# Starting a scan direction's preparation one block earlier in the SSD stage of a four-layer Mamba / ConvNeXt kernel

## The chip, the cores and the metric

The kernel runs on one core of a Trainium2 chip. The metric is the device time of one launch in microseconds (us), from the first to the last instruction of the core. A core has five engines that run side by side, each with its own list of instructions in a fixed order: PE (TensorE, matmuls; PEld is its weight load), DVE (VectorE), ACT (ScalarE), POOL (GpSimd) and SP (SyncE), which here issues all the DMAs. They wait for one another by semaphores.

## What is computed

The input is a float32 image batch (4, 96, 64, 64). It passes through four layers: a two-layer Mamba block with fusion and batch statistics, an SSD (Mamba-2) layer, another Mamba block, and a ConvNeXt block (7x7 depthwise convolution, layer norm, MLP). Only the SSD layer matters here. Cut to its core it is

```python
xn = rmsnorm(x)                                  # over channels, per pixel
xs = stack([xn, flip(xn), swap(xn), flip(swap(xn))])   # four scan directions, 4096 tokens each
z, xBC, dt = split(xs @ in_proj_w.T)             # 192, 192 + 128 + 128, 3 heads
dt  = softplus(dt + dt_bias)                     # step sizes, one per token and head
xBC = silu(conv_b + causal_conv4(xBC))           # x, B, C
dAc = cumsum(dt * A)  within a chunk
y   = tril(C B^T * exp(dAc_s - dAc_t)) * dt @ x  +  C exp(dAc) @ state  +  D * x
state = exp(dAc_last) * state + sum(exp(dAc_last - dAc) * dt * B x)
out = unscan(rmsnorm(y * silu(z)) @ out_proj_w.T) / 4 + residual
```

The decay factors of a whole direction depend on `dt` alone, and so on `xn` alone: they can be made before the direction's scan starts.

## The kernel before, in words

The program is written in a tile framework: the program's order gives each instruction its priority, a scheduler puts the instructions of each engine into a list, and tiles of a pool with one name share a ring of `bufs` buffers. A tile that takes a buffer of its ring waits until the readers of the buffer's tile before have finished.

`Ssd.run` (line 986) works through 16 directions: 4 images `b`, two orientations `o` (rows, columns), and two senses `r` (0 forward, 1 backward). A direction has four blocks of 1024 tokens, a block eight chunks of 128 tokens (`Q`), so 512 chunks in all. The loop of line 1021 runs over the chunks `n` and issues for each the recurrent work, in a software pipeline: `sums_to` (line 846, one DMA per pair of chunks that spreads the decay rows over the partitions, four chunks ahead), `decay` (856, two ahead), `weights` (869, one ahead), `outputs` (888), then `scale`, `by_channels` and `finish`. Line 931, in `outputs`, is a Square on ACT that runs once per chunk.

Two Python generators are advanced between these stages.

- `front` (line 780) makes the inputs of the next block: for `r` = 0 first `z` (16 matmul instructions, L796), then B and C (24, L814), then x (48, L825), then a Silu and the transposes of B. It is advanced four times per chunk (eight times where the next block is the first of a forward direction) and drained at the block's last chunk. Its PSUM tiles come from `bank("front")`, a ring of two.
- `prelude` (line 763) prepares the next direction. It exists once per direction, and its parts are:

```python
if r == 0:
    yield from self.rmsnorm(b) if o == 0 else self.turn()   # 8 steps
    yield from self.step_sizes(o)                           # 8 rows, a DMA read, the softplus
self.seq[b, o, r] = self.decays(r)
```

`rmsnorm` (666) loads and normalises an image into `xn[0]`; `turn` (685) copies `xn[0]` transposed to `xn[1]` on POOL. `step_sizes` (696) makes eight rows of `dt` (matmul L706, ACT copy L711, DMA L712 to a DRAM tile), reads them back in another shape (DMA L717), takes the softplus (from L719) and transposes the result (L725). `decays` (729) makes the cumulative sums (L743, L745), their exponentials, `coef` (L751 to L753) and the decay rows in DRAM (L756, L758, DMA L760). These matmuls too write to `bank("front")`: one tile for L725, one for L743 and L745 (read last by L748), one for L756. The tiles `dac`, `dec`, `edac`, `coef` of `decays` have two buffers each, so that those of a direction overwrite those of two directions before.

For a forward direction (`r` = 0) the prelude has 18 yields and so needs 19 calls of `next`; for a backward one it has none and one call does it all. Lines 1028 to 1033 decide when it is called: once per chunk from a first block on, and whatever is left is run at once at the last chunk of the third block (n = 23 of the direction ahead of it). The block after that is the one in which `front` makes the first block of the new direction.

Of the kernel before, what the change touches and what calls it, by code (L numbers as in the profile page):

```python
# [65 lines left out]
QB = BLK // Q  # L66
# [207 lines left out]
class Scan:  # L274
# [108 lines left out]
    def run(self, steps, wts, front, first):  # L383

        units = [(j, q, p) for j in range(3) for q in range(NQU) for p in range(2)]
        made = [first] + [{} for _ in steps[1:]]
        groups = [
            dict(
                pair=pair, sub=sub, c=c, wt=wts[sub], made=made[n], j=j, q=q, half=p, quarters=(p, p + 2),
                first=(q == 0 and p == 0), last=(q == NQU - 1 and p == 1),  # L390
                dma=(q % 2 == 0 and p == 1),
            )
            for n, (pair, sub, c) in enumerate(steps) for j, q, p in units
        ]
        total, each = len(groups), len(units)
        ahead = iter(())
        for n in range(-4, total + 6):
            slot = (n + LEAD) % each
            if slot == 0:
                for _ in ahead:  # L400
                    pass
                step = (n + LEAD) // each + 1
                ahead = front(step, made[step]) if step < len(steps) else iter(())

            def at(lag):
                return groups[n - lag] if 0 <= n - lag < total else None

            if (g := at(3)) and g["last"]:
                self.close(g)
            for stage, lag in (  # L410
                (self.load, -4), (self.spread, -1), (self.decay, -2), (self.scan, 0), (self.sums, 2),
            ):
                if g := at(lag):
                    stage(g)

            for lag, what in ((4, self.project), (5, self.fuse)):
                if (g := at(lag)) and g["last"] and g["j"] and (g["sub"] or lag == 4):
                    what(g, g["j"] - 1)
            for _ in range(PACE[slot] if slot < len(PACE) else 0):
                next(ahead, None)  # L420
# [152 lines left out]
class Ssd:  # L573
# [412 lines left out]
    def run(self):  # L986
        nblk = L // BLK
        steps = [
            (b, o, r, blk if r == 0 else nblk - 1 - blk)
            for b in range(B) for o in range(2) for r in range(2) for blk in range(nblk)  # L990
        ]
        made = [{} for _ in steps]
        chunks = []
        for n, (b, o, r, blk) in enumerate(steps):
            for m in range(QB):
                pair = {} if m % 2 == 0 else pair
                chunks.append(dict(
                    b=b, o=o, r=r, blk=blk, c=m if r == 0 else QB - 1 - m, made=made[n], pair=pair,
                    first=(m == 0 and n % nblk == 0), last=(m == QB - 1 and n % nblk == nblk - 1),
                    second=(m % 2 == 1),  # L1000
                ))

        def front(n):
            if n >= len(steps):
                return iter(())
            return self.front(*steps[n], made[n], steps[n + 1] if n + 1 < len(steps) else None)


        preludes = [
            (n, self.prelude(*steps[n][:3])) for n in range(0, len(steps), nblk)  # L1010
        ]
        first = preludes.pop(0)[1]
        for _ in range(2):
            next(first)
        self.weights_of(self.w)
        for _ in first:
            pass
        self.switch(0)
        for _ in front(0):
            pass  # L1020
        for n in range(-4, len(chunks) + 4):
            def at(lag):
                return chunks[n - lag] if 0 <= n - lag < len(chunks) else None

            m = n // QB + 1
            if n % QB == 0 and n >= 0:
                ahead = front(m)
            if n >= 0 and preludes and n // QB >= preludes[0][0] - 3:
                if n == (preludes[0][0] - 1) * QB - 1:
                    for _ in preludes.pop(0)[1]:  # L1030
                        pass
                else:
                    next(preludes[0][1], None)


            extra = m < len(steps) and steps[m][2:] == (0, 0)
            for point, stage in enumerate(("weights", "outputs", "finish", "decay")):
                if stage == "weights" and n >= 0 and n % QB == QB - 1 and m < len(steps):
                    while "silu" not in made[m]:
                        next(ahead)  # L1040
                if stage == "weights" and (g := at(-1)):
                    self.weights(g)
                if stage == "outputs" and (g := at(0)):
                    self.outputs(g)
                if stage == "outputs" and (g := at(1)) and g["second"]:
                    self.scale(g)
                if stage == "weights" and (g := at(3)) and g["second"]:
                    self.finish(g)
                if stage == "finish" and (g := at(2)) and g["second"]:
                    self.by_channels(g)  # L1050
                if stage == "decay" and (g := at(-4)) and not g["second"]:
                    self.sums_to(g)
                if stage == "decay" and (g := at(-2)):
                    self.decay(g)
                if n >= 0:
                    for _ in range(2 if extra else 1):
                        next(ahead, None)
            if n % QB == QB - 1 and n >= 0:
                for _ in ahead:
                    pass  # L1060
        self.switch(None)
# [250 lines left out]
```

## Time and profile before

| | us |
|---|---|
| three runs, median (lowest, highest) | 10018.94 (10013.64, 10032.7) |
| profiled run | 10004.88 |
| span of its core | 10002.8 |
| PE busy in the span | 8588.6 (86%) |
| DVE busy | 8164.7 (82%) |
| POOL busy | 6969.7 (70%) |
| ACT busy | 5524.9 (55%) |
| granted TensorE clock, mean | 0.935 |

The SSD layer lies in the middle, from 3068.6 to 6245.7 us. A window of the profile gives, for a stretch of time, the busy time of each engine with the count of its instructions, the clock that TensorE was granted (1.00 is full speed), the mean busy share of the DMA engines and what they moved in GB/s. A line of the timeline gives start, duration, engine (a `q` behind the name is the engine's sequencer, as for issuing a DMA), line of the code, the operation, the tiles written and read, and in brackets how long the engine had been idle and who ended that. Busy time is an average over stages with different limits, so the SSD stage is read by itself.

### The profile page before, as it was taken

What the parts mean: (1) busy time and instruction counts of PE and PEld (TensorE: products, weight loads), DVE (VectorE), ACT (ScalarE), POOL (GpSimd) and SP (SyncE); (2) the same over time, 40 slices, a digit from 0 to 9 for tenths busy, and PEclk for the clock granted to TensorE, in tenths of its full rate; (3) what the DMA queues carried; (4) which work ended last, traced back from release to release, by engine and by line L of the source; (5) the groups of instructions that cost most, each with busy time, mean ns of one, the idle gap of its engine ahead of it and who ended that gap; (6) DMA issues with size and microseconds to landing.
All of it is one profiled execution on the core that took longest, in us unless ns stands there. A gap on an engine that the chain in (4) does not pass through costs nothing. (4 is left out here: it accounts for less than half of the span.)

```text
span 10002.8 us, 109739 instructions
## 1 busy us (share of the span) xinstructions
PE 8588.6 (86%) x32744; PEld 3547.4 (35%) x32744; DVE 8164.7 (82%) x10861; ACT 5524.9 (55%) x10500; POOL 6969.7 (70%) x4600
## 2 busy tenths in 40 slices
PE   7888888888886988988998888788888888888688
PEld 1222222222213676776776766122121222221122
DVE  7999999999994666666656667799999999999787
ACT  5666666656653455545545544566666665665244
POOL 6888888888884555555555555688888888888322
PEclk9999999999997999999999999899999999999798
DMA  7777777777773223222312321767777777777442
GB/s 188 199 202 202 203 208 207 201 201 206 200 201 113 70 68 95 67 66 83 84 60 74 86 66 53 189 197 206 205 201 205 208 201 202 205 205 198 113 99 73
DMA packets 803534, 1528.27 MB, mean 153 GB/s; under 512 B 124253, under 2 KB 128249, under 8 KB 802170
## 3 DMA queue, kind: packets, MB, share of 16 engines
q1 hardware_dynamic: 802938, 1521.25, 54.7%
q8 instruction: 260, 4.26, 0.2%
q14 instruction: 336, 2.75, 0.1%
HBM read 1229.69 MB, written 156.37 MB: 139 GB/s over the span
## 5 line engine op out<-in xcount | busy, mean ns | idle before, releaser
L342 POOL TENSOR_TENSOR hc<-hs,bc 128x1024 f32<-128x1024 f32 x1536 | 3607.7, 2355 | 625.0 <-DVE hs L340 555.7
L340 DVE TENSOR_TENSOR_SCAN hs<-da,carry,bs 128x512 f32<-128x512 f32 x2016 | 2467.2, 1265 | 79.6 <-DVE bs L335 1.9
L107 ACT ACTIVATE da<-da,w_a 128x512 f32<-128x512 f32 x2304 | 1616.0, 716 | 1272.5 <-DMA da<-dd 1212.9
L361 PE MATMUL py<-hc,selsum 128*32 128x512 f32 x6144 | 1794.2, 636 | 472.8 <-POOL hc L342 462.9
L313 PE MATMUL bs<-du,seldu 64*128 64x512 f32 x4608 | 1578.0, 678 | 203.9 <-DVE hs L340 190.8
L335 DVE TENSOR_TENSOR bs<-bs,bc 128x1024 f32<-128x1024 f32 x1152 | 1398.3, 1214 | 189.3 <-PE bs L313 187.5
L308 POOL TENSOR_TENSOR du<-du,bc 128x1024 f32<-128x1024 f32 x384 | 904.4, 2355 | 289.6 <-DMA du<-dg 170.0
L361 PEld LDWEIGHTS py<-hc,selsum 128*32 128x32 f32 x6144 | 240.0, 110 | 1818.5 <-POOL hc L342 1119.0
L313 PEld LDWEIGHTS bs<-du,seldu 64*128 64x128 f32 x4608 | 446.5, 196 | 1205.2 <-DVE hs L340 859.4
L879 POOL TENSOR_TENSOR seg<-seg,cb 128x384 f32<-128x384 f32 x512 | 514.1, 1005 | 511.2 <-DVE cb L878 389.1
L194 PE MATMUL pu<-h,w_conv 96*128 96x512 f32 (+3 forms) x2048 | 834.5, 628 | 6.8 <-ACT rs L107 6.5
L863 DVE TENSOR_SCALAR seg<-dr,dac 128x128 f32<-128x128 f32 x1536 | 618.5, 435 | 265.1 <-PE y L908 248.0
L340 DVE TENSOR_TENSOR_SCAN hs<-bs,carry,du 128x512 f32<-128x512 f32 x672 | 823.8, 1260 | 8.5 <-issue 5.2
L814 PE MATMUL front<-pk,sconv 128*128 128x512 f32 x1536 | 750.2, 607 | 11.9 <-ACT z L802 7.5
L883 POOL TENSOR_TENSOR xs<-pre,coef 128x576 f32<-128x576 f32 x512 | 598.1, 1173 | 200.8 <-PE halves L922 144.4
L918 POOL TENSOR_TENSOR y<-y,xs 128x192 f32<-128x192 f32 x496 | 294.3, 593 | 546.7 <-DVE y L917 543.6
L931 ACT ACTIVATE y<-yz 128x192 f32<-128x192 f32 x512 | 186.1, 364 | 864.1 <-DVE yz L930 863.1
L825 PE MATMUL front<-sconv,pk 128*128 128x192 f32 x3072 | 573.8, 330 | 50.5 <-DVE pre L830 43.1
L1175 DVE SCALAR_TENSOR_TENSOR acc<-pad,c_conv,acc 96x1024 f32<-96x1024 f32 x336 | 491.4, 1467 | 112.1 <-ACT acc L1166 61.2
L345 ACT COPY carry<-hs 128x2 f32<-128x2 f32 x1344 | 250.5, 186 | 561.0 <-DVE hs L340 558.1
L825 PEld LDWEIGHTS front<-sconv,pk 128*128 128x128 f32 x3072 | 498.6, 191 | 81.1 <-DVE pre L830 68.9
L107 ACT ACTIVATE bs<-da,w_a 128x512 f32<-128x512 f32 x768 | 522.0, 680 | 2.3 <-DVE hs L340 0.7
(196 smaller groups left out, 13919.2 us busy)
## 6 DMA issues: line engine op xcount, KB each, us to landing
da<-dd SPq DMA_DIRECT2D x3072, 256.0 KB
du<-dg SPq DMA_DIRECT2D x768, 256.0 KB
dr<-rows SPq DMA_DIRECT2D x256, 384.0 KB
bc<-rows SPq DMA_DIRECT2D x256, 256.0 KB
dd<-delta SPq DMA_DIRECT2D x192, 256.0 KB
dg<-du SPq DMA_DIRECT2D x192, 256.0 KB
pk<-xn SPq DMA_DIRECT2D x128, 384.0 KB
pk<-xn SPq DMA_DIRECT2D x128, 256.0 KB
```

The source lines that it names most:

```text
L107: self.last = self.scalar.activation(out, in_, func, **kw)
L194: nc.tensor.matmul(pu[r0:r1], lhsT=wt["conv"][:kk, tap, d0:d1], rhs=h[:kk, b, ds(tap, T)], start=(tap == 0), stop=(tap == 3),)
L308: nc.gpsimd.tensor_tensor(g["du"], g["du"], self.b_or_c(g, 0), ALU.mult)
L313: nc.tensor.matmul(g["bs"][:, i], lhsT=self.sel["du"][rows, g["half"], g["q"]], rhs=g["made"]["du"][rows, g["j"]], start=True, stop=True,)
L335: nc.vector.tensor_tensor(dbx, dbx, self.b_or_c(g, 0), ALU.mult)
L340: nc.vector.tensor_tensor_scan(hs[:, i], da[:, i], dbx[:, i], init, ALU.mult, ALU.add)
L342: nc.gpsimd.tensor_tensor(g["hc"], hs, self.b_or_c(g, 1), ALU.mult)
L361: nc.tensor.matmul(py[rows], lhsT=self.sel["sum"][:, g["q"]], rhs=g["hc"][:, i], start=(g["q"] == 0), stop=(g["q"] == NQU - 1),)
L814: nc.tensor.matmul(p, lhsT=self.conv[:, i, DI + q * DST : DI + (q + 1) * DST], rhs=pk[:, i, ds(c * T, T)], start=(i == 0), stop=(i == 2),)
L825: nc.tensor.matmul(p, lhsT=pk[:, i, ds(c * Q, Q)], rhs=self.conv[:, i, :DI], start=(i == 0), stop=(i == 2),)
L863: nc.vector.tensor_scalar(seg[:, h], g["pair"]["dr"][:, c % 2 * NH + h], made["dac"][:, n0 + h : n0 + h + 1], 0.0, ALU.subtract, ALU.min,)
L883: nc.gpsimd.tensor_tensor(xs, x.to_broadcast([P, 3, NH, HD]), coef.to_broadcast([P, 3, NH, HD]), ALU.mult)
```

## The change

One number in the condition that decides from which block on the prelude is advanced. With `preludes[0][0]` the number of the first block of the direction to prepare, the prelude was advanced from three blocks before that on (the second block of the direction ahead); now it is from four blocks before (the first block). The drain at the last chunk of the third block stays.

```diff
             m = n // QB + 1
             if n % QB == 0 and n >= 0:
                 ahead = front(m)
-            if n >= 0 and preludes and n // QB >= preludes[0][0] - 3:
+            if n >= 0 and preludes and n // QB >= preludes[0][0] - 4:
                 if n == (preludes[0][0] - 1) * QB - 1:
                     for _ in preludes.pop(0)[1]:
                         pass
                 else:
                     next(preludes[0][1], None)
```

There are 15 preludes that this concerns; that of the first direction runs ahead of the loop.

## The prediction

> **What bounds the kernel now.** I read, in this order: the page (which stages there are), the windows view by direction and by block (where the SSD stage takes longer than its like), and the timeline of one slow block, once for all engines and once for SP alone. The window edges are the starts of the Square of line 931, one per chunk; I call the 16 directions D0 to D15 (even ones run forward, r = 0; odd ones backward, r = 1), their blocks 0 to 3, and their chunks 0 to 31.
>
> ```profile
> span 10002.8 us, 109739 instructions
> ```
>
> The SSD stage runs from 3068.6 to 6245.7 us, 3177 us; the change touches nothing else. Over it PE is busy 2786 us of 3177, more than any other engine (DVE 2049), so an idle or half-clocked PE is time lost. By direction, D5, D6 and D7:
>
> ```profile
> 4144.70:4345.10 200.40, 180.20 (x928) 138.62 (x927) 121.05 (x324) 94.76 (x221) 102.43 (x126) 0.91 0.22 62
> 4345.10:4525.20 180.10, 161.57 (x918) 128.67 (x918) 128.21 (x331) 92.34 (x213) 104.32 (x127) 0.99 0.26 73
> 4525.20:4740.90 215.70, 187.62 (x943) 142.67 (x941) 136.61 (x340) 111.15 (x248) 112.00 (x134) 0.91 0.28 80
> ```
>
> Columns: window, length, busy PE, PEld, DVE, ACT, POOL, then clock and DMA. Odd directions take 200.4 (they prepare by `turn`) or 215.7 us (by `rmsnorm`), even ones 180 to 184; the clock is 0.91 in D5 and D7 and 0.99 in D6. D5 block by block, then the first block of D6, which like D5's last has a z part in its front beside the chunks, then blocks 0 and 1 of D7:
>
> ```profile
> 4144.70:4188.60 43.90, 40.01 (x225) 31.71 (x224) 31.55 (x82) 21.78 (x53) 24.97 (x31) 0.96 0.25 72
> 4188.60:4232.50 43.90, 39.85 (x215) 31.06 (x215) 31.58 (x80) 20.84 (x50) 25.81 (x32) 0.92 0.27 73
> 4232.50:4287.30 54.80, 50.75 (x252) 35.05 (x250) 30.67 (x80) 24.66 (x55) 27.59 (x35) 0.91 0.16 46
> 4287.30:4345.10 57.80, 49.58 (x241) 40.79 (x241) 27.25 (x85) 27.48 (x65) 24.06 (x30) 0.85 0.22 63
> 4345.10:4392.60 47.50, 42.40 (x241) 34.41 (x240) 34.16 (x93) 24.17 (x59) 27.33 (x35) 0.96 0.28 76
> ...
> 4525.20:4569.00 43.80, 38.18 (x220) 29.85 (x218) 33.60 (x82) 22.16 (x53) 25.67 (x32) 1.00 0.27 73
> 4569.00:4625.80 56.80, 45.72 (x242) 34.77 (x242) 42.37 (x95) 35.64 (x74) 35.17 (x41) 0.97 0.43 122
> ```
>
> See four things. `turn` in block 1 costs nothing (43.9 with and without it). `rmsnorm` there costs 13.0 us (56.8 against 43.8). The eight `step_sizes` rows cost 10.9 in block 2, and the whole of it is PE busy time (50.75 less 39.85). Block 3 does no preparation by the program's order, yet is 10.3 us longer than D6's block 0 with the same number of PE instructions (241). SP's timeline over D5's blocks 2 and 3 (start, duration, engine, line, what), then that of all engines, then two windows in it, say why:
>
> ```profile
> 4276.64 2.66 SPq L712 DMA_DIRECT2D dtrows<-dtrow  x2
> 4280.46 0.57 SPq L717 DMA_DIRECT2D dtx<-dtrows  x1
> 4299.40 0.31 SPq L760 DMA_DIRECT2D rows<-row  x1
> 4300.90 2.59 SPq L850 DMA_DIRECT2D dr<-rows  x4
> ```
>
> ```profile
> 4290.16 0.29 ACT L719 ACTIVATE ua<-dtx 96x128 f32<-96x128 f32 x1
> ...
> 4298.92 0.26 DVE L748 TENSOR_TENSOR wt<-front,dac 128x96 f32<-128x96 f32 x1 [1.08 <-ACT dec L107]
> ...
> 4300.10 3.32 PE L796 MATMUL front<-inw,xn 96*128 96x192 f32 x16
> ...
> 4322.69 1.15 POOL L883 TENSOR_TENSOR xs<-pre,coef 128x576 f32<-128x576 f32 x1 [20.99 <-PE halves L922]
> ```
>
> ```profile
> 4278.40:4300.10 21.70, 18.36 (x97) 16.82 (x96) 15.04 (x44) 10.27 (x34) 16.18 (x21) 0.74 0.01 4
> 4300.10:4321.50 21.40, 21.40 (x89) 15.11 (x89) 5.91 (x23) 5.04 (x11) 0.76 (x1) 0.98 0.25 76
> ```
>
> Before, the preparation takes 15 steps, at chunks 8 to 22, and needs 19; the rest is drained at chunk 23: row 8, the DRAM round trip (L712, L717), the softplus, the transpose, `decays`. From 4278.4 to 4300.1 PE gets chunks and this tail, no front work, at a mean clock of 0.74; the next direction's front starts only then, since its first tile follows the tail's three in the ring of two "front" banks and so waits until L748 has read the second of them. Then the front runs alone for 21.4 us (POOL busy 0.76), the chunks also having waited for the `dr` loads behind L760 on SP's queue. What is interleaved elsewhere is done here one after the other.
>
> **What the Trainium skill says.** "Perfetto Trace Analysis", Optimization Strategy: a gap that repeats on the engine to be saturated can mean that there is no room for the next tile. The trace agrees: the ring of two "front" banks, in all seven such places. "TensorE: Matmul & The Clock Gate", Part 1: the clock falls to half after an idle window and comes back after a busy one. The trace agrees in kind: 0.74 in the thin stretch, 0.98 in the dense one. "PSUM — Partial Sum Buffer", Engine vs sequencer instructions: matmuls run in program order, the other engines' queues are strict FIFO. That is why a held front also holds what stands behind it; L796 starting 0.9 us after L748's end agrees.
>
> **The change part by part.** Preparation starts at chunk 0 instead of 8. Steps at chunks 0 to 22 are 23; the long preparations need 19 and the short ones (odd direction next: `decays` only) 1. No instruction is added or removed.
>
> (a) `turn` (8 POOL copies, 4 directions) and `rmsnorm` (3 directions, with its loads and stores on SP) go to block 0 of the odd direction. Blocks 0 and 1 are alike (43.9, 43.9), so each costs there what it cost in block 1: nothing, and 13.0. What they write, xn, was last read in the direction before or earlier. Net 0.
>
> (b) The rows go from block 2 to block 1, each with its PE, ACT and SP step: minus 10.9, plus about 10.5, as the last two ran at half clock before (two L706 pairs at 0.93 us each against 0.51). Net -0.4.
>
> (c) The tail goes to chunks 16 (L717), 17 (softplus), 18 (transpose, `decays`). Its PE work is one L725, two L743, two L745, one L756: 0.42 + 2 x 0.39 + 2 x 0.45 + 0.42 = 2.5 us at the low clock they had. On SP, L717 and L760 now precede the `dr` loads for chunk 22, which have a lead of two chunks. Nine conv matmul steps of the front (3 banks) are ahead of the tail in the ring; the fourth bank waits for L748. L717 to L748 took 18.7 us here (4280.46 to 4299.18); three banks and their chunks carry about 2.3 chunks of 5.5 us, 12.5 us. So the front is held some 6 us. In block 3 a hold of 21.7 us cost about 10.3, half; 6 us gives 3. Lower bound 0 (the front has 23 items, four per chunk, done by the sixth chunk of eight, so a hold of two chunks can be made up); upper bound 11, a full stall as now. I take +2 for PE and +3 for the hold: block 2 becomes 44 + 5 = 49.
>
> (d) Block 3 loses the stall: from 57.8 to that of a block with z. D6's block 0 is 47.5; its blocks 1 and 2 are 45.8 and 44.5. I take 46: -11.8. Bounds: -9 and -13.3.
>
> (e) Even directions: `decays` goes from chunk 8 to chunk 0, past nothing but the block's own front. It costs 1.3 in block 1 now (45.8 against 44.5). In block 0 it overwrites dac, dec, edac and coef of the direction before, read last at chunks 30 and 31, so ACT may wait for the last readers. Unknown: -0.5 to +2; I take +0.5.
>
> Sum by its own span: a `turn` direction from 43.9 + 43.9 + 54.8 + 57.8 = 200.4 to 43.9 + 54.4 + 49 + 46 = 193.3, -7.1. An `rmsnorm` direction (D7: 43.8, 56.8, 56.0, 59.1) to 56.8 + 55.6 + 49 + 46 = 207.4, -8.3. Four and three of them: -53. Eight even ones: +4. Total -49, so 9954 on the span of 10002.8. The profiled run took 10004.9, the three runs have a median of 10018.9; on that scale 9970.
>
> **The rivals.** *All recovered.* The hold of (c) is made up in the slack: block 2 is 46, even directions 0, the clock nearer 1. 3 more in seven directions and the 4: -74, and with (d) at its bound -85: 9934. For it: even directions hide the same `decays`. Against: the tail is longer than `decays`.
>
> *The stall moves.* The hold in block 2 is as long as the one at the turn of direction now, because 9.7 us of the 18.7 are between L717 and L719 and may not shrink; the front then runs alone at the end of block 2. Block 2 takes +11 more than 44 and the gain is eaten: 10019, with 10000 to 10040. For it: same ring, same chain. Against: three banks ahead of the tail, five chunks behind it.
>
> *Slower.* The mechanism is (e): at chunk 0 the ring of banks is taken by `decays`, which waits for chunk 31, while the front there has a z part and the pipeline of the new direction is just filling. If each even direction gets a stall as in block 3 (11.8), 8 x 11.8 = 94 against 49 gained: 10064. It decides from 6.1 us per even direction on. For it: the front's first bank is behind `decays`. Against: at chunk 8 the same order costs 1.3 us, and the readers waited for are one chunk old.
>
> *It does nothing* can't be: the 15 steps become 19 by the counts.
>
> **How the numbers follow.** Likeliest (-49): 0.60, own range 9940 to 9999. All recovered: 0.10. The stall moves: 0.18. Slower: 0.12. About 0.2% (20 us) is what a measurement of this kernel can tell from no change. Faster than 9999: 0.60 + 0.10 + 0.02 of the third = 0.72; within: 0.15; slower: 0.12 + 0.01 = 0.13. The range 9925 to 10035 leaves out the slower case and the tails.
>
> **What would show it.** Right: odd directions of about 193 and 207 us with a clock above 0.95; no stretch of block 3 without front matmuls; L717 in chunk 16, L760 by chunk 20; POOL's 21 us wait gone. Step (c) wrong: block 2 above 52 and a new wait for L748 there. Step (e) wrong: even block 0 above 50. The prediction fails if block 3 keeps its stall without a tail, as then something at the turn of direction itself makes it.

## The result and the profile after

| | before | after |
|---|---|---|
| median of 6 runs each, us | 10016.29 (10005.11 to 10032.7) | 9943.95 (9935.35 to 9972.6) |
| ratio, 95% interval | | 0.9931 (0.9916 to 0.9947) |
| span of the profiled run, us | 10002.8 | 9939.0 |

The change saves 72 us by the medians, 64 us between the two profiled spans. First the page's head, then the windows of the directions D5, D6 and D7 of the changed kernel (window, length, busy PE, PEld, DVE, ACT, POOL, clock, DMA share, GB/s):

```profile
span 9939.0 us, 109693 instructions
```

```profile
4130.30:4317.60 187.30, 169.96 (x921) 129.04 (x920) 122.84 (x327) 94.31 (x223) 101.36 (x125) 0.95 0.24 67
4317.60:4498.80 181.20, 164.03 (x916) 130.60 (x915) 126.36 (x328) 92.47 (x210) 104.34 (x127) 0.97 0.25 72
4498.80:4710.10 211.30, 184.28 (x946) 136.81 (x945) 144.39 (x343) 111.23 (x251) 111.53 (x135) 0.94 0.29 82
```

D5 (a `turn` preparation) went from 200.4 to 187.3 us, D6 from 180.1 to 181.2, D7 (`rmsnorm`) from 215.7 to 211.3. Now D5 by blocks, and blocks 0 and 1 of D7:

```profile
4130.30:4172.50 42.20, 38.88 (x218) 30.27 (x217) 29.34 (x82) 21.56 (x53) 24.90 (x31) 0.96 0.28 75
4172.50:4226.70 54.20, 50.44 (x237) 33.04 (x236) 31.95 (x82) 24.97 (x57) 27.15 (x34) 0.91 0.21 61
4226.70:4273.00 46.30, 42.16 (x242) 34.70 (x241) 34.46 (x92) 24.46 (x60) 26.95 (x35) 0.96 0.24 70
4273.00:4317.60 44.60, 38.48 (x227) 31.02 (x226) 27.09 (x75) 23.33 (x55) 22.36 (x27) 1.00 0.23 64
4498.80:4558.20 59.40, 50.41 (x251) 37.34 (x249) 43.81 (x98) 37.22 (x79) 32.15 (x39) 0.91 0.41 117
4558.20:4617.80 59.60, 52.48 (x231) 32.40 (x231) 37.09 (x82) 27.28 (x60) 30.11 (x36) 0.91 0.25 72
```

Block 3, at 57.8 us with a clock of 0.85 before, takes 44.6 at full clock. Of these 13.2 us PE's busy time makes up 11.1 (49.58 to 38.48) and its idle time 2.1 (8.2 to 6.1). The rows of `step_sizes` have moved from block 2 to block 1 with their PE time, and what is left in block 2, the tail, lengthens it to 46.3. SP's timeline and PE's around the start of D5's block 2 (4226.7) show the tail:

```profile
4222.62 0.57 SPq L717 DMA_DIRECT2D dtx<-dtrows  x1
4233.05 0.35 SPq L850 DMA_DIRECT2D dr<-rows  x1
4237.73 0.33 SPq L760 DMA_DIRECT2D rows<-row  x1
```

```profile
4232.74 0.27 PE L725 MATMUL front<-ident,dtx 96*128 96x96 f32 x1
...
4234.96 1.02 PE L814 MATMUL front<-pk,sconv 128*128 128x512 f32 x2
...
4237.04 0.27 PE L756 MATMUL front<-ident,dac 128*96 128x128 f32 x1
...
4237.70 2.74 PE L814 MATMUL front<-pk,sconv 128*128 128x512 f32 x6
```

The front's L814 goes on between the tail's matmuls; its longest pauses there are 2.1 us (4232.8 to 4235.0) and 1.7 us. In the kernel before, the front stood still for the 21.7 us of the prediction's last fence.

The lengths of the blocks, taken as the time between starts of the per-chunk Square in the timeline and averaged over each kind of direction, are the measure for all that follows. Each row is from one profiled execution.

| us | turn (4): blocks 0 to 3 | sum | rmsnorm (3): blocks 0 to 3 | sum | even (8), sum |
|---|---|---|---|---|---|
| before | 43.9 44.1 54.9 57.6 | 200.4 | 44.4 57.3 55.9 58.1 | 215.7 | 181.6 |
| after | 43.7 52.6 46.8 44.8 | 187.8 | 60.5 59.9 46.6 44.8 | 211.8 | 181.7 |
| start early, drain kept (e2) | 43.9 52.6 46.3 57.2 | 199.9 | 60.6 59.3 46.4 57.8 | 224.0 | 180.0 |
| start as before, no drain (e1) | 43.1 53.1 48.3 44.4 | 188.9 | 45.3 62.0 47.5 44.3 | 199.1 | 183.2 |
| start at chunk 4 (e3) | 42.7 48.6 51.5 44.2 | 187.0 | 49.8 60.2 52.4 43.9 | 206.2 | 182.3 |
| drain kept, tail in another ring (e8) | 42.6 44.1 54.0 48.4 | 189.0 | 45.1 59.2 55.8 48.6 | 208.8 | 180.0 |
| e1 and e8 together (e11) | 42.2 53.1 47.6 44.3 | 187.3 | 44.5 60.1 47.8 44.3 | 196.7 | 179.6 |

By this table the change gave 4 x 12.6 = 50 us in the `turn` directions, 3 x 3.9 = 12 in the `rmsnorm` ones, and nothing in the even ones: 62, of the 64 between the spans. The last digits are not firm: over all the traces the even directions lie between 179.6 and 184.1 us, also where an edit does not touch them.

### The profile page after: what moved, and what is told of

Same layout as the page of the kernel before. It is cut to its first block, busy times and chain, and to the rows that moved or that the text cites. A ratio compares the mean times of both kernels' runs of the same rounds, so it can differ in the third digit from the quotient of the medians.

```text
span 9939.0 us, 109693 instructions
## 1 busy us (share of the span) xinstructions
PE 8555.7 (86%) x32744; PEld 3519.5 (35%) x32744; DVE 8200.3 (83%) x10861; ACT 5528.2 (56%) x10500; POOL 6968.8 (70%) x4600
## 5 line engine op out<-in xcount | busy, mean ns | idle before, releaser
L313 PE MATMUL bs<-du,seldu 64*128 64x512 f32 x4608 | 1570.6, 676 | 208.8 <-DVE hs L340 193.0
L863 DVE TENSOR_SCALAR seg<-dr,dac 128x128 f32<-128x128 f32 x1536 | 645.6, 454 | 276.3 <-PE y L908 269.1
L814 PE MATMUL front<-pk,sconv 128*128 128x512 f32 x1536 | 756.7, 610 | 24.5 <-ACT z L802 20.4
L1175 DVE SCALAR_TENSOR_TENSOR acc<-pad,c_conv,acc 96x1024 f32<-96x1024 f32 x336 | 491.8, 1467 | 110.5 <-ACT acc L1166 59.2
```

What stands on the lines that cost most here:

```text
L313: nc.tensor.matmul(g["bs"][:, i], lhsT=self.sel["du"][rows, g["half"], g["q"]], rhs=g["made"]["du"][rows, g["j"]], start=True, stop=True,)
L814: nc.tensor.matmul(p, lhsT=self.conv[:, i, DI + q * DST : DI + (q + 1) * DST], rhs=pk[:, i, ds(c * T, T)], start=(i == 0), stop=(i == 2),)
L863: nc.vector.tensor_scalar(seg[:, h], g["pair"]["dr"][:, c % 2 * NH + h], made["dac"][:, n0 + h : n0 + h + 1], 0.0, ALU.subtract, ALU.min,)
L1175: nc.vector.scalar_tensor_tensor(acc, images[b % 2][:, y : y + rows, x : x + WW], wt["conv"][:, tap : tap + 1], acc, ALU.mult, ALU.add,)
```

## The experiments

Two theories. *Tail*: the gain comes from no longer issuing the end of the preparation right in front of the next direction's front. *Room*: it comes from spreading the preparation over more chunks. The change does both at once; the first two experiments do one each.

**e1: the tail earlier, the start as before.**

```diff
                 else:
-                    next(preludes[0][1], None)
+                    for _ in range(2 if n % (4 * QB) < 2 * QB else 1):
+                        next(preludes[0][1], None)
```

(in the kernel before, where preparation begins with the second block)

> The preparation starts with the second block, as before, but takes two steps per chunk in that block, so that its tail (DMA read, softplus, decays) falls at chunks 16 to 18, as in the changed kernel, and nothing is left for the drain. Theory 'tail': the gain comes from the tail no longer standing in front of the next direction's front in the ring of two front banks; then block 3 of the odd directions is about 45 us, as in the changed kernel, and the time is 9935 to 9965, a ratio of 0.992 to 0.995. Rival 'room': the gain comes from spreading the preparation over two blocks; then the crowded second block gives most of it back and the time is 10000 or more.

Measured: 9926.6 us, ratio 0.992 (0.9896 to 0.9944). Block 3 of D5:

```profile
4256.80:4301.10 44.30, 38.59 (x229) 31.44 (x228) 26.26 (x71) 23.25 (x54) 22.14 (x27) 1.00 0.22 63
```

All of the gain without an earlier start, a little more even than *tail* expected. The crowded second block takes 53 and 62 us, hardly more than the same steps cost when spread: over blocks 0 to 2 a `turn` direction takes 144.5 us against 143.1 in the changed kernel, an `rmsnorm` one 154.8 against 167.0.

**e2: the start earlier, the tail as before.**

```diff
-                else:
+                elif n % (4 * QB) < 15:
                     next(preludes[0][1], None)
```

(in the changed kernel)

> The preparation starts with the first block, as in the changed kernel, but stops after 15 steps, so that the same four steps as before are left for the drain at chunk 23. Theory 'tail': no gain, 10005 to 10030, and block 3 of the odd directions stays at 57 to 58 us. Rival 'room': most of the gain, 9940 to 9970, though the drain is there.

Measured: 10002.84 us, ratio 0.9991 (0.9978 to 1.0004), no difference. Block 3 of D5 has its stall and its low clock:

```profile
4300.50:4355.80 55.30, 47.17 (x243) 38.55 (x242) 28.58 (x88) 27.55 (x66) 23.43 (x30) 0.88 0.23 67
```

*Room* has fallen. The gain comes from where the preparation ends. Beginning earlier gives none, and in this trace the `rmsnorm` directions even pay 8.3 us each for it (224.0 against 215.7).

**e8: the same drain, but its PSUM tiles in another ring.** This tests why the drain is costly.

```diff
-        pt = self.bank("front")[:, :n]
+        pt = self.bank("out")[:, :n]
...
-        ps = self.bank("front")
+        ps = self.bank("out")
...
-        pt = self.bank("front")[:n, :Q]
+        pt = self.bank("out")[:n, :Q]
```

> The kernel before, with the drain where it was, but the PSUM tiles of the tail (transpose of the step sizes, cumulative sums, transpose of the decay rows) come from the ring 'out' instead of 'front'. Theory 'ring': the next direction's front no longer waits for the tail, runs beside the chunks from 4278 on, and the time falls by 30 to 65 us (9950 to 9985). Rival 'SP queue': the chunks still wait for the dr loads behind the write of the decay rows, and block 3 stays at 57 us: 10005 to 10030. Rival 'the ring out then holds the chunks': slower than 10030.

Measured: 9911.82 us, ratio 0.9899 (0.9878 to 0.992). Three lines of its timeline in D5, of all engines and of SP:

```profile
4259.70 1.30 PE L796 MATMUL front<-inw,xn 96*128 96x192 f32 x7
...
4260.77 0.57 SPq L717 DMA_DIRECT2D dtx<-dtrows  x1
```

```profile
4273.05 0.31 SPq L760 DMA_DIRECT2D rows<-row  x1
```

The front's first matmuls (L796) now start before the tail's DMA read is issued, 13 us ahead of its last write. In the kernel before they started 19.6 us after L717. Nothing but the name of three PSUM tiles differs, so the ring of two banks was the hold. The gain is above the range expected. Block 3 of D5:

```profile
4265.90:4314.10 48.20, 41.39 (x245) 32.87 (x245) 28.80 (x82) 26.65 (x63) 24.20 (x31) 1.00 0.26 76
```

The tail is still in this block, and PE runs 245 instructions where it ran 241 before. Yet it is busy for 41.39 us instead of 49.58, at a clock of 1.00 instead of 0.85, and idle for 6.8 instead of 8.2. So most of what the hold cost here, 8.2 of 9.6 us, was not an idle PE but matmuls that took longer at the low clock (L725: 0.42 us before, 0.30 here). Even directions take 180.0 us instead of 181.6. Their `decays` leaves that ring as well, but e2, which keeps it there, has 180.0 too, so that this part is the ring's is not shown.

**e9: the tail's DMAs off SP's queue.** In the kernel before, L717 and L760 are issued with `nc.scalar.dma_start`.

> The kernel before, but the read of the step sizes (L717) and the write of the decay rows (L760) are issued from ACT's DMA queue, so that SP no longer holds the dr loads of the chunks behind them. Theory 'ring': the front of block 3 still waits for the tail in the ring, block 3 of the odd directions stays within 3 us of 57.6: 10000 to 10025. Rival 'SP queue': block 3 falls to 50 or less, 9965 or less. Possible harm: ACT waits for the row copy with its own queue.

Measured: 10013.01 us, ratio 0.9995 (0.9988 to 1.0002). Block 3 of D5 stays as it was:

```profile
4289.80:4348.90 59.10, 51.72 (x245) 42.55 (x243) 27.86 (x85) 27.28 (x64) 23.85 (x30) 0.83 0.21 62
```

The `dr` loads that queued behind L760 were not what held the block.

**e12: both.** The ring of e8 and the queue of e9.

> The tail at the drain as before, its PSUM tiles in the ring 'out', and L717 and L760 on ACT's DMA queue. With the ring 'out' alone block 3 of the odd directions is 48.5 us, 3.7 above the changed kernel. If that rest is SP's queue (dr loads behind L760), block 3 falls to 45 and the time by 20 to 25 us against the ring alone, to 9885 to 9895. If it is the tail's own PE and DVE work (about 3 us), nothing changes: 9905 to 9920.

Measured: 9919.33 us, ratio 0.9896 (0.9878 to 0.9914), no faster than e8; block 3 stays at 48.3 us. So the 3.6 us by which e8's block 3 exceeds the changed kernel's are not SP's queue. In D5 (48.2 against 44.6 us) 2.9 of them are PE busy time, with 18 more instructions, both at full clock: the block has more work in it, the tail's included.

**e3: the latest start that leaves no drain.**

```diff
-            if n >= 0 and preludes and n // QB >= preludes[0][0] - 3:
+            if n >= 0 and preludes and n >= (preludes[0][0] - 4) * QB + 4:
```

> All preparations start at chunk 4, the latest start at which 19 steps leave nothing for the drain; DMA read, softplus and decays fall at chunks 20, 21 and 22. Theory 'tail' with the hold in the ring as its price: decays at chunk 22 still holds the ring when the next direction's front begins, some 10 us of the former 21.7, so a third to a half of the gain is lost: 9960 to 9985. If only the presence of the drain mattered, 9945 as in the changed kernel or better, since the rmsnorm directions have their copies of turn less bunched.

Measured: 9934.32 us, ratio 0.9931 (0.9913 to 0.9948), as the changed kernel; the first expectation, a loss of a third to a half, missed. With the DMA read at chunk 20 and `decays` at chunk 22 block 3 is 44.2 us. So an end at chunk 22 is early enough. The timeline of D5 shows how it fits. The block's own front ends with L842 at 4241.1, the tail's PSUM tiles run from L725 (4244.79) to L748 (4249.3), and the next front's L796 starts at 4250.46, 7 us before block 3. The read of the step sizes is issued at 4226.11, and ACT waits for it:

```profile
4229.32 0.31 ACT L719 ACTIVATE ua<-dtx 96x128 f32<-96x128 f32 x1 [0.56 <-DMA dtx<-dtrows]
```

That is 3.2 us after its issue; in e1 it is 2.2 to 3.2. In the kernel before, 9.7 us lay between the two, and L719 (4290.16) had no idle ACT before it: it stood in ACT's list behind the chunks' work. So the greater part of these 9.7 us was the order of that list and not the DMA.

**e4: `rmsnorm` preparations at chunk 4, the others at chunk 0.**

> As the changed kernel, but preparations with rmsnorm start at chunk 4 and all others at chunk 0. In the changed kernel the eight POOL copies of turn for the same image run at chunks 8 to 10 of the rmsnorm directions, right behind rmsnorm and two directions ahead of their place in the program, and chunk 9 takes 18 us there. If this bunching is what made these directions gain only 2 to 5 us each instead of 8, they gain 5 us each more here (9930). If the ring hold by a tail at chunks 20 to 22 costs more than that, they lose 3 to 6 us each (9955 to 9965).

Measured: 9935.6 us, ratio 0.9928 (0.9905 to 0.995). The `rmsnorm` directions fell from 211.8 to 207.2 us each, about the 5 us expected (14 us for the three), though the time of the runs cannot tell this from the changed kernel.

**e5, e6, e7: one kind of preparation early at a time.**

```diff
+            early = 4 if preludes and steps[preludes[0][0]][1:3] == (1, 0) else 3
-            if n >= 0 and preludes and n // QB >= preludes[0][0] - 3:
+            if n >= 0 and preludes and n // QB >= preludes[0][0] - early:
```

(e5; e6 has `(0, 0)`, e7 `[2] == 1`)

> Only the preparations of the forward directions with swapped axes (turn, four of the fifteen) start with the first block. By the directions of the two traces they gave 50 us of the 64: the time should be 9960 to 9975, a ratio of 0.994 to 0.996. If the gain came from the rmsnorm or the backward preparations, it is 10000 or more.

> Only the preparations with rmsnorm (three of the fifteen) start with the first block. By the traces they gave 12 us: 9998 to 10012, block 3 of their directions at 45 us and blocks 0 and 1 at 60 us each. Rival: the 60 us in blocks 0 and 1 came from the other moves, and then this alone gives 25 us, as predicted (9990).

> Only the preparations of the backward directions (decays alone, eight of the fifteen) start with the first block. By the traces the even directions changed by 1 us in all: 10010 to 10022, no difference. Rival: they cost 0.5 us each as predicted (+4), or help by releasing the ring earlier (-10).

Measured: e5 9967.47 us, 0.995 (0.9929 to 0.997), as expected; e6 9984.65 us, 0.9971 (0.9963 to 0.998), a gain of 29 us by the medians, which is the rival's 25 rather than the 12 expected; e7 10004.23 us, 0.9993 (0.9982 to 1.0004), no difference. In the trace of e6 the `rmsnorm` directions are those of the changed kernel (60.0, 60.5, 47.1 and 44.3 us, 211.9), 11 us for the three; the span of its profiled run is 9999.8 us, the median of its runs 15 less. Where its runs gain the rest is not located, so what these directions contribute stays open between 11 and 29 us.

**e10: the changed kernel without the copies of `turn`.**

```diff
-            self.nc.gpsimd.tensor_copy(
+            if b == 0: self.nc.gpsimd.tensor_copy(
```

> The changed kernel without the 24 POOL copies of turn for images 1 to 3 (8 in each rmsnorm direction, where the scheduler puts them); part of the computation is left out. Theory 'bunched turn': blocks 0 and 1 of the rmsnorm directions, 60.5 and 59.9 us, lose 8 to 12 us together, mostly at chunk 9, now 18 us: 9910 to 9920. Rival: POOL is not what holds these blocks, they stay at 118 to 120 us together and the time at 9935 to 9945. The turn directions themselves do not change in either case, as no copy of turn runs in them.

Measured: 9913.56 us, ratio 0.9901 (0.9878 to 0.9923). Blocks 0 and 1 of D7:

```profile
4469.70:4527.10 57.40, 48.58 (x251) 37.24 (x249) 41.76 (x98) 37.18 (x79) 29.89 (x37) 0.94 0.41 121
4527.10:4581.10 54.00, 50.52 (x230) 31.87 (x230) 33.72 (x82) 27.20 (x61) 24.47 (x30) 0.94 0.29 79
```

111.4 us against 59.4 + 59.6 = 119.0: the eight copies cost 7.6 us there (8.5 in the mean of the three directions), though POOL is busy for half of these blocks only. They run in chunks 7 to 9, within 16 us. The copies overwrite `xn[1]`, which this direction still reads in its first block (`pk` loads from 4530.8 to 4540.5 in D7; the first copy is at 4551.0).

**e11: the two best edits together**, e1's two steps per chunk and e8's ring.

> The two fastest edits together: two steps of the preparation per chunk in the second block (no drain left) and the tail's PSUM tiles in the ring 'out'. If the ring's hold is the only price of the tail, the second edit adds to the first only what the tail still costs in block 2 (47.5 to 48.3 against 44): 7 directions by 1 to 3 us, 9900 to 9925. If the two edits cure the same thing and nothing else, no difference from the faster of them (9912).

Measured: 9876.98 us, ratio 0.9858 (0.9836 to 0.988). Its interval lies below those of the changed kernel (0.9916 to 0.9947) and of e1, and just touches that of e8. Both expectations missed: it is faster than either. The `rmsnorm` directions have a block 3 without a tail and keep their cheap order (196.7 us). But of the 43 us between the SSD stages of e1's trace and this one, 29 come from the even directions (183.2 to 179.6 each), 7 from the `rmsnorm` and 6 from the `turn` ones. That the freed ring makes the even directions faster would fit, but is not shown, as they vary by as much without it.

## Why the prediction was right

The forecast was 9970, faster, in a range of 9925 to 10035; 9943.95 came. The mechanism, that the drained tail holds the ring of "front" banks while the next direction's front waits, is shown by e1, e2 and e8; that SP's queue added to it is not borne out (e9, e12). The sizes, by the steps of the prediction:

- **(d), block 3.** Forecast 57.8 to 46, measured in the mean 57.6 and 58.1 to 44.8: -12.8 and -13.3, near the far bound of -13.3. The block runs at a clock of 1.00.
- **(c), the tail in block 2.** Forecast 49, measured 46.8 and 46.6. The +2 for its PE work was about right and the +3 for a hold was not: L717 to L748's end is 14.9 us (4222.62 to 4237.51), and 10.1 of it come before L725, while the front's banks ahead of the tail in the ring are still to be filled. The 9.7 us from L717 to L719 that "may not shrink" are 5.8 here and 3.2 in e3.
- **(b), the rows.** Forecast +10.5 in block 1, measured +8.5 in the `turn` directions (44.1 to 52.6).
- **(a), the first eight steps.** Forecast net 0; this step failed in the `rmsnorm` directions, though the sum hardly shows it. Block 0 became 60.5 instead of 56.8 and block 1 59.9 instead of 55.6. Two readings of it were wrong. "`turn` in block 1 costs nothing" rested on D5's block 1, but no copy of `turn` runs in D5: the scheduler had put the copies two directions ahead, into D3, D7 and D11, beside `rmsnorm`, both before and after. And `xn[1]` was not free at chunk 0: it is read in block 0 of the `rmsnorm` direction. Before, the copies were spread over 63 us between the steps of `rmsnorm`; now all eight fall at its end, within 16 us. Without them (e10) the two blocks take 111.9 us, where 112.4 was forecast and 120.4 came. Why `rmsnorm` without copies still costs 14 us in block 0 (58.3 in e10's mean), when with them it cost 13 in block 1, stays open.
- **(e), the even directions.** Forecast +0.5, measured +0.1, and e7 shows no difference. But the step priced something that does not happen there. In the kernel before, D7's `decays` runs in D6's block 0 (L743 at 4384.17, L748 at 4388.62), not in block 1. In the changed kernel the scheduler puts it into block 3 of D5, ahead of its place in the program:

```profile
4303.64 0.46 PE L743 MATMUL front<-da,tri 128*128 128x96 f32 x2
...
4314.33 0.27 ACT L107 ACTIVATE edac<-dac 128x96 f32<-128x96 f32 x1
4315.56 0.24 DVE L748 TENSOR_TENSOR wt<-front,dac 128x96 f32<-128x96 f32 x1
```

From L743 to L748 it now takes 12 us instead of 4.7, as the wait for the last readers that (e) feared would suggest. What this costs is part of block 3's 44.8. Block 1 of the even directions stays at 46.2 us in the mean, so the 1.3 us read as the price of `decays` there were not its price.

Together: a `turn` direction gained 12.6 instead of 7.1 us, an `rmsnorm` one 3.9 instead of 8.3. The rival "all recovered" (9934) comes nearest, and was right about block 2 (46), block 3 (its bound) and the even directions (0). It fails where the forecast does, in (a): by its steps an `rmsnorm` direction takes 202.9 us (56.8 + 55.6 + 46 + 44.5), and 211.8 came. So the nearness of 9970 to 9944 is in part luck: about 36 us more than forecast were gained in (b) to (e), and 24 were lost in (a). "The stall moves" and "slower" did not come about: block 2 stays under 52, even block 0 at 47.8.

## What to carry to other kernels

A short piece of serial work costs little by itself and much by its place: ahead of a long generator that takes tiles from the same ring of buffers, it holds that generator for its whole latency, with its DMA round trip and its waits in other engines' lists. Ask which ring its tiles come from and what stands behind it in that ring; another ring (here three names) or an earlier end cures it, an earlier beginning does not. And look in the trace where moved work runs before pricing its move: a scheduler may have placed it somewhere else than the program's order says, as here the copies of `turn` and the `decays` of the backward directions.

## What had not been expected of the hardware

The granted clock had a mean of 0.74 in the stretch of the kernel before in which PE was busy 18.4 of 21.7 us (first window of the prediction's last fence). In the changed kernel's block 3 PE shows nearly the same busy share (38.5 of 44.6 us) at full clock. So the busy share of a long stretch does not tell which clock is granted; it is also raised by the low clock itself, at which the same matmul takes longer (L725: 0.42 against 0.27 us).

The few microseconds before a fall tell more. The records of the clock in this trace last 3.4 us or multiples of it, all but one. Around that stretch it fell to half at 4273.54 and at 4294.02, and these are the 3.4 us before:

```profile
4270.12:4273.54 3.42, 1.05 (x6) 0.57 (x5) 3.42 (x7) 1.26 (x5) 2.94 (x4) 1.00 0.26 80
4290.60:4294.02 3.42, 1.37 (x9) 1.08 (x9) 3.41 (x8) 2.34 (x10) 3.42 (x6) 1.00 0.00 0
```

PE was busy for 31% and 40% of them. The clock fell 57 times in the SSD stage of this trace, each time after 3.4 us in which PE had been busy for 21% to 69%. Of the stretches of this length that full clock followed, none had less than 45%; between 45% and 69% both occurred.
